# A last stage in the place of the spectral matrices: residual loaded once, columns on SBUF partitions 22 to 105, last exchange on two queues

## Chip, core and metric

The kernel runs on one core of one Trainium2 chip, as one program of some 61,000 instructions. The metric is the device time of a run in microseconds (us), the lower the better. The core has five engines that work in parallel, each from its own queue in order: PE (matrix products), DVE and ACT (element by element), POOL (the same, used here for fills and small copies) and SP (which here only issues transfers). Transfers between DRAM and SBUF, the on-chip memory of 128 partitions, are issued from SP and ACT and carried out by the core's DMA engines.

## What is computed

The input is an image of 4 x 56 x 56 positions with 128 channels. Layer 0 is group normalization, local attention over 7 x 7 windows and a residual sum. Layer 1 works on the 3136 positions of each image as a sequence t: a linear attention with a residual sum, then a sum of a spectral filter and a short autoregressive filter, again with a residual sum.

```python
x = x + conv_attention(group_norm(x))            # 7x7 windows, 4 heads
t = to_tokens(x)                                 # (4, 3136, 128)
t = t + linear_attention(layer_norm(t))
u = layer_norm(t)
# for the one scale that log_weights + gumbel select:
#   U_plus, U_minus = causal FFT convolutions of u with 16 filters phi
#   out = sum_k sigma_k^0.25 (U_plus_k Mpp_k + U_minus_k Mpm_k)
#   out = out + sum_{i<3} shifted(u, i) Mu_i
t = t + out * weight                             # cut to T // frac positions
```

The end of the kernel, which the change touches, is the last sum: the spectral part is brought back from the frequency domain to positions and added to what is there already, the residual `td`.

## The kernel before

`layers` does everything up to the spectral filter. It leaves in DRAM `td` (residual with the autoregressive part, 4 images x 3136 positions x 128 channels), `xd` (the rows of the image, transformed), the filter's values `vd` and the matrices `wd`. Its instructions are put in order by a hand-written planner; the change does not touch it.

`spectral_layer` (L1420) goes over N1 = 42 frequencies `m1`, most of them in pairs (`UNITS`), and its PE order is written out by hand (`manual_schedule`); the order on the other engines is found by the framework from what it expects to be ready, with the order of the code as priority. It keeps in a pool `sp1`, for its whole length, `mats` (16 KB a partition, L1431), `gt` (112 KB, L1441), the filter matrices of the frequencies in work, and three `us` (10.5 KB each, L1445). For each frequency it

- loads `xm` from `xd` (`load_tokens`) and makes `us` (`token_points`);
- makes the matrices of the next frequencies into `gt` (`matrices`, PE L1519, copies L1529) in turn with the products of this one (`product`, PE L1539), whose result is copied to `ys` by ACT (L1631);
- exchanges axes through DRAM (`regroup`): four stores `yd<-ys` (L1552), and after their landing four loads `yg<-yd` (L1558), all on SP's queue;
- some steps later, in `results`, transforms columns (`columns`, PE L1567), copies to `zs` with ACT and DVE (`evacuate`, L182 and L184) and stores `zd<-zs` in four transfers on SP's queue (`store_columns`, L1582).

The last frequency, 41, has nothing left to hide behind: its exchange, columns and stores are followed only by the last stage.

`onto_the_rest` (L1678) is that last stage, in a new pool `fin` and a new PSUM pool of four banks, opened when the pools of `spectral_layer` are closed. `zd` holds, for each of 56 image columns, 84 values (real and imaginary parts of 42 frequencies) x 2 x 512. The stage goes through the columns of the two halves of the image (28 each) in eleven steps of 1, 1, 2, 4, 4, 4, 4, 4, 2, 1, 1 columns. In each step and for each half `q`,

- ACT's queue loads the residual `tl<-td` (L1707), 56 rows on the partitions from 64q on, four buffers;
- SP's queue loads `z<-zd` (L1709), 84 rows on partitions 0 to 83, four pairs of buffers;
- PE multiplies with `onto` (L1717), four products a column for the two halves, over all 128 partitions; the partitions from 64 on of the z buffers are filled with zeros once before (L1695, half by DVE, half by POOL), as is `onto` (L1685);
- DVE adds the result, masked, to `tl` (L1726);
- ACT's queue stores `out_dram<-tl` (L1731).

Two lines say how a z load is laid out:

```python
z = zs[n % 4][q]
nc.sync.dma_start(z[: 2 * N1, :wc], zd[ws].rearrange("w p s b e -> p w s (b e)"))
```

Of the kernel before, what the change touches and what calls it, by code (L numbers as in the profile page):

```python
# [11 lines left out]
F32 = mybir.dt.float32  # L12
AF = mybir.ActivationFunctionType
ALU = mybir.AluOpType
AX = mybir.AxisListType

P = 128
B, H, W, C = 4, 56, 56, 128
# [39 lines left out]
NS, BR = 2, H // 2  # L58
N1, N2, NM = 42, W, W // 2
# [5 lines left out]
NSB = NS * B  # L65
# [68 lines left out]
def hybrid_kernel(  # L134
# [23 lines left out]
    nc = tc.nc  # L158
    xt = x.rearrange("b h w c -> b (h w) c")
    ot = out.rearrange("b h w c -> b (h w) c")  # L160
# [3 lines left out]
    table = {k: nc.inline_tensor(v, name=k).ap() for k, v in spectral_tables().items()}  # L164
# [1255 lines left out]
    def spectral_layer():  # L1420


        with ExitStack() as ph:
            tabs = ph.enter_context(tc.tile_pool(name="tabs", bufs=2))
            sp = ph.enter_context(tc.tile_pool(name="sp", bufs=2))
            sp1 = ph.enter_context(tc.tile_pool(name="sp1", bufs=1))
            ps_g = ph.enter_context(tc.tile_pool(name="ps_g", bufs=1, space=bass.MemoryType.PSUM))


# [118 lines left out]

            def regroup(m1, ys):

                for j in range(4):
                    nc.sync.dma_start(  # L1552
                        yd[m1, j::4].rearrange("n k e -> k n e"), ys[32 * j : 32 * (j + 1)]
                    )
                yg = sp.tile([P, NSB, C], F32, name="yg")
                for at, p, part in parts():
                    k0 = (2 * p + part) * NSB
                    nc.sync.dma_start(yg[at], yd[m1, :, k0 : k0 + NSB])  # L1558
                return yg

            def columns(m1, yg, zs, pz):
# [14 lines left out]

            def store_columns(m1, zs):
                to = zd.rearrange("(c p) r s b e -> c p r s (b e)", p=2)
                for s in range(NS):
                    for part in range(2):  # L1580
                        at = 64 * s + NM * part
                        nc.sync.dma_start(to[:, :, part * N1 + m1, s], zs[at : at + NM])  # L1582

            turn = [0]

# [22 lines left out]
            def step(s):  # L1608


                one = UNITS[s - 1] if s else []
                two = UNITS[s] if s < len(UNITS) else []
                turns = NM // 4
                free = MQ * len(one)

                order = list(range(free, NQE)) + list(range(free)) if two else []
                need = lambda t: -(-NMQ * (t + 1) // 4) if t < free else 0
                done = 0

                def make():  # L1620
                    if order and need(order[0]) <= done:
                        t = order.pop(0)
                        for n in range(len(two)):
                            matrices(s, t, n)

                def use(q, ns):

                    py = bank().rearrange("p (n c) -> p n c", c=C)
                    for i, n in enumerate(ns):
                        product(py[:, i], s - 1, us_of(one[q]), q, n)  # L1630
                    nc.scalar.copy(ys[:, ns[0] : ns[-1] + 1], py[:, : len(ns)])  # L1631

                if not one:
                    load_to(1)
                    points(0)
                    while order:
                        make()
                elif len(one) == 1 and two:
                    ys = sp.tile([P, turns, C], F32, name="ys")
                    for n in range(turns):  # L1640
                        make()
                        use(0, [n])
                        done += 1
                        if n == 3:
                            points(two[0])
                    ygs[one[0]] = regroup(one[0], ys)
                    make()
                    points(two[1])
                else:
                    waiting = list(ygs)  # L1650
                    for q in range(len(one)):
                        ys = sp.tile([P, turns, C], F32, name="ys")
                        for n in range(0, turns, 2):
                            last = n + 1 == turns
                            if last and q == 0 and two:
                                points(two[0])
                            if last and q == len(one) - 1:
                                if q:
                                    waiting.append(one[0])
                                for m1 in waiting:  # L1660
                                    results(m1)
                            use(q, [n] if last else [n, n + 1])
                            done += len(range(n, min(n + 2, turns)))
                            make()
                        ygs[one[q]] = regroup(one[q], ys)
                    if len(two) == 2:
                        points(two[1])
                assert not order

            with tc.manual_schedule(engines={mybir.EngineType.PE}):  # L1670
                for s in range(len(UNITS) + 1):
                    if s + 1 < len(UNITS):
                        tables_of(UNITS[s + 1][0])
                    step(s)
                for m1 in list(ygs):
                    results(m1)

    def onto_the_rest():  # L1678

        with ExitStack() as ph:  # L1680
            fin = ph.enter_context(tc.tile_pool(name="fin", bufs=4, reuse_waits="tile"))
            ps_o = ph.enter_context(tc.tile_pool(name="ps_o", bufs=4, space=bass.MemoryType.PSUM))

            onto = fin.tile([P, NS, 64], F32, name="onto", bufs=1)
            nc.vector.memset(onto, 0.0)  # L1685
            nc.scalar.dma_start(
                onto[: 2 * N1, :, :H], table["onto"].rearrange("p (s h) -> p s h", s=NS)
            )
            zs = [
                [fin.tile([P, 4, NS, B * C], F32, name=f"z{q}{i}", bufs=1) for q in range(2)]  # L1690
                for i in range(4)
            ]
            for i in range(4):
                for q, e in enumerate((nc.vector, nc.gpsimd)):
                    e.memset(zs[i][q][64:], 0.0)  # L1695
            rows_in = td.rearrange("b (h w) c -> h b w c", w=W)
            rows_out = ot.rearrange("b (h w) c -> h b w c", w=W)

            steps = (1, 1, 2, 4, 4, 4, 4, 4, 2, 1, 1)
            assert sum(steps) == W // 2  # L1700
            for n, wc in enumerate(steps):
                w0 = sum(steps[:n])
                tl = fin.tile([P, B, max(steps), C], F32, name="tl")
                zin = []
                for q in range(2):
                    ws = slice(q * BR + w0, q * BR + w0 + wc)
                    nc.scalar.dma_start(tl[64 * q : 64 * q + H, :, :wc], rows_in[:, :, ws])  # L1707
                    z = zs[n % 4][q]
                    nc.sync.dma_start(  # L1709
                        z[: 2 * N1, :wc], zd[ws].rearrange("w p s b e -> p w s (b e)")  # L1710
                    )
                    zin.append(z)
                for i in range(wc):
                    po = ps_o.tile([P, B, C], F32, name="po2")
                    for s in range(NS):
                        for q in range(2):
                            nc.tensor.matmul(  # L1717
                                po[64 * q : 64 * (q + 1)].rearrange("p b c -> p (b c)"),
                                onto[:, s],
                                zin[q][:, i, s],  # L1720
                                start=(s == 0),
                                stop=(s == NS - 1),
                            )
                    for q in range(2):
                        at = slice(64 * q, 64 * q + H)
                        nc.vector.scalar_tensor_tensor(  # L1726
                            tl[at, :, i], po[at], hmask[at], tl[at, :, i], ALU.mult, ALU.add
                        )
                for q in range(2):
                    ws = slice(q * BR + w0, q * BR + w0 + wc)  # L1730
                    nc.scalar.dma_start(rows_out[:, :, ws], tl[64 * q : 64 * q + H, :, :wc])  # L1731

    unfit = keep.tile([1, 1], mybir.dt.int32, name="unfit")
    layers(False, unfit)
    bad = nc.values_load(unfit)
    spectral_layer()
    onto_the_rest()
    with tc.If(bad > 0):
        layers(True, None)
        spectral_layer()  # L1740
        onto_the_rest()


# [52 lines left out]
```

## Time and profile before

| what | before |
| --- | --- |
| median of three runs | 1659.32 us (1655.94 to 1659.87) |
| the profiled execution, its own time | 1652.25 us |
| its span, first to last instruction | 1650.4 us |
| PE busy | 1452.0 us, 88% of the span |
| DVE, ACT, POOL busy | 1012.8, 753.8, 419.2 us |
| mean granted clock of PE | 0.927 |
| moved by DMA | 207.21 MB, 126 GB/s over the span |
| last product of frequency 41 (L1539) begins | 1494.86 us |
| first residual load `tl<-td` issued | 1509.41 us |
| first load `z<-zd` issued | 1516.70 us |
| PE on the last stage (L1717) | 75.1 us busy, 224 records |
| DVE's sums on the last stage (L1726) | 56 of 750 ns |

Times in the profile run from the start of the span. L1717 stands for line 1717 of the program. A group of instructions is named by engine, line and operation with out<-in by tile names. "SPq" and "ACTq" are the queues of SP and ACT, where transfers are issued; a transfer itself stands as "DMA out<-in". The chain of waits is followed back from the last instruction: at each step to what released it, or to what stood before it on its engine. A window gives, for a stretch of the span, the busy time of each engine, PE's granted clock, the mean busy share of 16 DMA engines and the bytes moved per second.

### The profile page before, as it was taken

The numbers are of one execution on the slowest core, as the hardware profiler recorded it, in microseconds if no ns is written. First come the engines' busy times: TensorE is split into PE (matmuls) and PEld (weight loads), VectorE is DVE, ScalarE is ACT, GpSimd is POOL, SyncE is SP. The second block draws the span as 40 slices with busy tenths as digits, with TensorE's granted clock in tenths as the row PEclk, the third lists the DMA queues.
The fourth block names the chain that finished last, engine by engine and source line by source line (L and its number), as shares of the span: only waits on it lengthen the run. The fifth ranks groups of instructions, "written<-read, shape, count | busy, mean of one in ns | idle before, by whom it ended". The sixth has DMA issues, their size and how long they took to land.

```text
span 1650.4 us, 61067 instructions
## 1 busy us (share of the span) xinstructions
PE 1452.0 (88%) x26361; PEld 1124.3 (68%) x26361; DVE 1012.8 (61%) x2056; ACT 753.8 (46%) x1599; POOL 419.2 (25%) x831
## 2 busy tenths in 40 slices
PE   4886888899999999884999999999999999992556
PEld 3665667766776676672888888888888888880211
DVE  4775778676876767540766666666666666642324
ACT  2342444355545544342656656565665665640000
POOL 4134326543753464340001010101010011003000
PEclk9698999899998999885999999999999999995888
DMA  6554454744434234357234345444454444435997
GB/s 174 117 103 106 87 92 107 156 119 122 120 93 126 68 113 119 86 142 189 66 99 128 104 117 136 123 116 114 122 133 111 115 123 123 113 89 142 224 262 225
DMA packets 294710, 207.21 MB, mean 126 GB/s; under 512 B 106272, under 2 KB 261376, under 8 KB 294432
## 3 DMA queue, kind: packets, MB, share of 16 engines
q1 hardware_dynamic: 281538, 189.64, 45.2%
q10 hardware_dynamic: 12894, 13.58, 3.1%
q8 instruction: 209, 3.42, 0.9%
q14 instruction: 69, 0.57, 0.1%
HBM read 115.49 MB, written 87.64 MB: 123 GB/s over the span
## 4 chain that ended last, share of the span: by engine, by line
PE 66%; DMA 13%; DVE 9%; POOL 5%; SPq 3%; issue 2%; ACT 1%; DVEq 0%; ACTq 0%; POOLq 0%
PE pg L1519 18%; PE pg L1539 17%; PE pg L1488 5%; PE results L1186 4%; PE bk L823 3%; PE scores L1156 3%; PE pg L1567 3%; PE bk L888 2%; SPq L230 2%; DVE e L1176 2%; DMA tl<-td 2%; DMA out_dram<-tl 2%; DMA z<-zd 2%; PE bk L728 2%; POOL hna L542 2%
## 5 line engine op out<-in xcount | busy, mean ns | idle before, releaser
L1529 DVE COPY gt<-pg 128x448 f32<-128x448 f32 x672 | 372.9, 617 | 225.8 <-PE pg L1519 225.7
L1529 ACT COPY gt<-pg 128x448 f32<-128x448 f32 x672 | 313.7, 555 | 100.8 <-PE pg L1519 100.5
L1519 PE MATMUL pg<-v,mats 32*128 32x224 f32 (+1 forms) x5632 | 308.4, 355 | 0.0
L1539 PE MATMUL pg<-gt,us 128*32 128x128 f32 x9408 | 297.9, 277 | 1.4 <-DVE gt L1529 1.3
L1539 PEld LDWEIGHTS pg<-gt,us 128*32 128x32 f32 x9408 | 256.4, 138 | 52.2 <-DVE gt L1529 45.4
L1519 PEld LDWEIGHTS pg<-v,mats 32*128 32x128 f32 x5632 | 250.0, 186 | 30.0 <-issue 28.2
L1500 POOL COPY us<-us 128x448 f32<-128x448 f32 x42 | 23.5, 560 | 671.8 <-DVE us L1497 611.7
L1172 ACT ACTIVATE e<-scores 126x768 f32<-126x768 f32 (+1 forms) x140 | 107.6, 768 | 113.0 <-PE scores L1156 76.1
L1176 DVE TENSOR_TENSOR e<-e,relb 126x768 f32<-126x768 f32 (+1 forms) x140 | 138.5, 990 | 23.6 <-ACT e L1172 23.2
L1200 DVE RECIPROCAL recs<-results 128x96 f32<-128x96 f32 (+1 forms) x140 | 99.5, 710 | 49.9 <-PE results L1186 48.5
L1717 PE MATMUL po<-z,onto 128*64 128x512 f32 x224 | 75.1, 720 | 59.9 <-DMA z<-zd 59.3
L1156 PEld LDWEIGHTS scores<-qT,kp 32*126 32x126 f32 (+1 forms) x2240 | 76.6, 189 | 51.3 <-ACT e L1172 24.0
L1156 PE MATMUL scores<-qT,kp 32*126 32x96 f32 (+1 forms) x2240 | 99.9, 293 | 12.4 <-ACT e L1172 12.0
L1631 ACT COPY ys<-pg 128x256 f32<-128x256 f32 (+1 forms) x171 | 58.6, 343 | 106.9 <-PE pg L1539 103.5
L1488 PE MATMUL pg<-tok,xm 56*128 56x56 f32 x1344 | 87.2, 278 | 21.7 <-DMA xm<-xd 21.7
L1488 PEld LDWEIGHTS pg<-tok,xm 56*128 56x128 f32 x1344 | 81.5, 191 | 34.9 <-issue 23.6
L1717 PEld LDWEIGHTS po<-z,onto 128*64 128x64 f32 x224 | 25.7, 162 | 110.2 <-issue 74.4
L1497 DVE COPY us<-pg 128x448 f32<-128x448 f32 x84 | 48.5, 620 | 71.7 <-PE pg L1488 71.7
L823 PE MATMUL bk<-mu,ut 128*112 128x128 f32 x672 | 87.5, 291 | 2.2 <-POOL ut L807 1.5
L1186 PE MATMUL results<-e,v_sb 126*32 126x96 f32 (+1 forms) x2240 | 77.4, 258 | 11.8 <-DVE aT L1201 11.6
L1726 DVE SCALAR_TENSOR_TENSOR tl<-po,hmask,tl 56x512 f32<-56x512 f32 x56 | 42.0, 750 | 74.1 <-PE po L1717 73.4
L823 PEld LDWEIGHTS bk<-mu,ut 128*112 128x112 f32 x672 | 82.7, 195 | 4.3 <-POOL ut L807 1.9
(175 smaller groups left out, 1942.7 us busy)
## 6 DMA issues: line engine op xcount, KB each, us to landing
xd<-xs SPq DMA_DIRECT2D x112, 168.0 KB
xm<-xd SPq DMA_DIRECT2D x168, 112.0 KB
yd<-ys SPq DMA_DIRECT2D x168, 112.0 KB
yg<-yd SPq DMA_DIRECT2D x168, 112.0 KB
zd<-zs SPq DMA_DIRECT2D x168, 112.0 KB
v_sb<-vpad SPq DMA_DIRECT2D x224, 63.0 KB
z<-zd SPq DMA_DIRECT2D x10, 1344.0 KB
acc<-in_x_dram SPq DMA_DIRECT2D x28, 224.0 KB
```

Source lines behind the costliest of these rows:

```text
L823: nc.tensor.matmul(pt[:CP, g * C : (g + 1) * C], ut[:, t0 : t0 + 2 * CP - 1 : 2], mu[:, i, :], start=(i == 0), stop=(i == NAR - 1),)
L1156: nc.tensor.matmul(sp[:, h, c * nq : (c + 1) * nq], keys_of(x0, y0 + c * KH, KH)[hs], qTs[b, ty][hs, QR * x0 : QR * x0 + nq], start=True, ...
L1172: nc.scalar.activation(e.rearrange("k (h q) -> k h q", h=NH), sp, AF.Exp)
L1176: nc.vector.tensor_tensor(e, e, relb[qc].rearrange("k h c q -> k (h c q)"), ALU.mult)
L1186: nc.tensor.matmul(po[hs, i, :nq], ones[:kn] if i else v_sb[:kn, c, hs], e[:, h, c], start=(c == 0), stop=(c == 1),)
L1200: nc.vector.reciprocal(rec, po[:, 1, :nq])
L1488: nc.tensor.matmul(pu[p][:, HALF * k : HALF * (k + 1)], xm[at, k // B, k % B, :], tok[at], start=True, stop=True,)
L1519: nc.tensor.matmul(pg[g][:, cols * i : cols * (i + 1)], mats[rows, t, ni * n + i, :], v[rows], start=True, stop=True,)
L1529: copy(rows_of(u + 1, t)[:, : MQ * nm, :, e0 : e0 + ni], pg[g][:, : cols * ni].rearrange("p (i q c) -> p q c i", i=ni, q=MQ * nm),)
L1539: nc.tensor.matmul(py[32 * j : 32 * (j + 1)], us.rearrange("p c k m -> p (c k) m")[:, NSB * FIRST[p, c] : NSB * (FIRST[p, c] + 4), 4 * n + j],
L1631: nc.scalar.copy(ys[:, ns[0] : ns[-1] + 1], py[:, : len(ns)])
L1717: nc.tensor.matmul(po[64 * q : 64 * (q + 1)].rearrange("p b c -> p (b c)"), onto[:, s], zin[q][:, i, s], start=(s == 0), stop=(s == NS - 1),)
```

## The change

The last stage becomes part of `spectral_layer`, and `onto_the_rest` goes.

- `sp1` (`mats`, `gt`, `us`) gets a stack of its own, `matrices_in`, and is closed right after the loop over the steps, before the results of the last frequencies. The pool `fin` is opened in its place, while the pools of tables, of `zs`/`yg` and the eight PSUM banks stay open.
- The residual is one tile, `rest`, of 56 KB a partition. It is loaded by fourteen transfers of four columns each, all issued on ACT's queue ahead, in the code, of the results of the last frequencies.
- `onto` and z loads lie on partitions 22 to 105 instead of 0 to 83. The z buffers are three pairs instead of four, filled with zeros whole, by POOL.
- The last stage's products take PSUM from the eight banks of `spectral_layer` (`bank()`) instead of four of their own. DVE adds into `rest`, and the stores to the output are made from it.
- For frequency 41 the exchange (`regroup`), and for 40 and 41 the stores to `zd` (`store_columns`), go half on SP's queue and half on ACT's.

The diff, cut:

```diff
-            sp1 = ph.enter_context(tc.tile_pool(name="sp1", bufs=1))
+            matrices_in = ph.enter_context(ExitStack())
+            sp1 = matrices_in.enter_context(tc.tile_pool(name="sp1", bufs=1))
...
             def regroup(m1, ys):
+                queues = (nc.sync, nc.sync if m1 < N1 - 1 else nc.scalar)
                 for j in range(4):
-                    nc.sync.dma_start(
+                    queues[j % 2].dma_start(
                         yd[m1, j::4].rearrange("n k e -> k n e"), ys[32 * j : 32 * (j + 1)]
                     )
...
-                    nc.sync.dma_start(yg[at], yd[m1, :, k0 : k0 + NSB])
+                    queues[part].dma_start(yg[at], yd[m1, :, k0 : k0 + NSB])
...
+                queues = (nc.sync, nc.sync if m1 < N1 - 2 else nc.scalar)
...
-                        nc.sync.dma_start(to[:, :, part * N1 + m1, s], zs[at : at + NM])
+                        queues[part].dma_start(to[:, :, part * N1 + m1, s], zs[at : at + NM])
...
+            matrices_in.close()
+            fin = ph.enter_context(tc.tile_pool(name="fin", bufs=1, reuse_waits="tile"))
...
+            rest = fin.tile([P, B, BR, C], F32, name="rest")
+            half = [slice(64 * q, 64 * q + H) for q in range(2)]
+            for w0 in range(0, BR, 4):
+                for q in range(2):
+                    nc.scalar.dma_start(
+                        rest[half[q], :, w0 : w0 + 4], rows_in[:, :, q * BR + w0 : q * BR + w0 + 4]
+                    )
+            among = slice(P // 2 - N1, P // 2 + N1)
+            onto = fin.tile([P, NS, 64], F32, name="onto")
+            nc.gpsimd.memset(onto, 0.0)
+            nc.scalar.dma_start(
+                onto[among, :, :H], table["onto"].rearrange("p (s h) -> p s h", s=NS)
+            )
+            DEEP = 3
+            zin = [
+                [fin.tile([P, 4, NS, B * C], F32, name=f"z{q}{i}") for q in range(2)] for i in range(DEEP)
+            ]
+            for zs in zin:
+                for z in zs:
+                    nc.gpsimd.memset(z, 0.0)
+            with tc.manual_schedule(engines={mybir.EngineType.PE}):
                 for m1 in list(ygs):
                     results(m1)
...
             for n, wc in enumerate(steps):
...
                     nc.sync.dma_start(
-                        z[: 2 * N1, :wc], zd[ws].rearrange("w p s b e -> p w s (b e)")
+                        zin[n % DEEP][q][among, :wc],
+                        zd[q * BR + w0 : q * BR + w0 + wc].rearrange("w p s b e -> p w s (b e)"),
                     )
...
-                    po = ps_o.tile([P, B, C], F32, name="po2")
+                    po = bank()
...
-                            tl[at, :, i], po[at], hmask[at], tl[at, :, i], ALU.mult, ALU.add
+                            rest[half[q], :, w0 + i],
+                            po[half[q]].rearrange("p (b c) -> p b c", b=B),
+                            hmask[half[q]],
+                            rest[half[q], :, w0 + i],
+                            ALU.mult,
+                            ALU.add,
...
-                    nc.scalar.dma_start(rows_out[:, :, ws], tl[64 * q : 64 * q + H, :, :wc])
+                    nc.scalar.dma_start(
+                        rows_out[:, :, q * BR + w0 : q * BR + w0 + wc], rest[half[q], :, w0 : w0 + wc]
+                    )
```

More of the change, by code (lines that the diff above doesn't have):

```diff
@@ L1674, in spectral_layer @@
                     step(s)
+            matrices_in.close()
+            fin = ph.enter_context(tc.tile_pool(name="fin", bufs=1, reuse_waits="tile"))
+            rows_in = td.rearrange("b (h w) c -> h b w c", w=W)
+            rows_out = ot.rearrange("b (h w) c -> h b w c", w=W)
+            rest = fin.tile([P, B, BR, C], F32, name="rest")
[5 more added lines that the diff above has]
+                    )
@@ L1675, in spectral_layer @@
+            with tc.manual_schedule(engines={mybir.EngineType.PE}):
                 for m1 in list(ygs):
                     results(m1)
[L1678 to L1697, printed above, removed]
@@ L1699, in onto_the_rest @@
             steps = (1, 1, 2, 4, 4, 4, 4, 4, 2, 1, 1)
-            assert sum(steps) == W // 2
+            assert sum(steps) == BR
             for n, wc in enumerate(steps):
                 w0 = sum(steps[:n])
-                tl = fin.tile([P, B, max(steps), C], F32, name="tl")
-                zin = []
                 for q in range(2):
-                    ws = slice(q * BR + w0, q * BR + w0 + wc)
-                    nc.scalar.dma_start(tl[64 * q : 64 * q + H, :, :wc], rows_in[:, :, ws])
-                    z = zs[n % 4][q]
@@ L1709, in onto_the_rest @@
                     nc.sync.dma_start(
-                        z[: 2 * N1, :wc], zd[ws].rearrange("w p s b e -> p w s (b e)")
+                        zin[n % DEEP][q][among, :wc],
+                        zd[q * BR + w0 : q * BR + w0 + wc].rearrange("w p s b e -> p w s (b e)"),
                     )
-                    zin.append(z)
                 for i in range(wc):
-                    po = ps_o.tile([P, B, C], F32, name="po2")
+                    po = bank()
                     for s in range(NS):
@@ L1717, in onto_the_rest @@
                             nc.tensor.matmul(
-                                po[64 * q : 64 * (q + 1)].rearrange("p b c -> p (b c)"),
+                                po[64 * q : 64 * (q + 1)],
                                 onto[:, s],
-                                zin[q][:, i, s],
+                                zin[n % DEEP][q][:, i, s],
                                 start=(s == 0),
@@ L1724, in onto_the_rest @@
                     for q in range(2):
-                        at = slice(64 * q, 64 * q + H)
                         nc.vector.scalar_tensor_tensor(
-                            tl[at, :, i], po[at], hmask[at], tl[at, :, i], ALU.mult, ALU.add
+                            rest[half[q], :, w0 + i],
[4 more added lines that the diff above has]
+                            ALU.add,
                         )
                 for q in range(2):
-                    ws = slice(q * BR + w0, q * BR + w0 + wc)
-                    nc.scalar.dma_start(rows_out[:, :, ws], tl[64 * q : 64 * q + H, :, :wc])
+                    nc.scalar.dma_start(
+                        rows_out[:, :, q * BR + w0 : q * BR + w0 + wc], rest[half[q], :, w0 : w0 + wc]
+                    )
     unfit = keep.tile([1, 1], mybir.dt.int32, name="unfit")
@@ L1736, in hybrid_kernel @@
     spectral_layer()
-    onto_the_rest()
     with tc.If(bad > 0):
@@ L1740, in hybrid_kernel @@
         spectral_layer()
-        onto_the_rest()
 def kernel(**inputs):
```

## The prediction

> **What bounds the kernel now.** I read the page first (where in the span the DMA engines are full), then the chain of waits from 1494 us on, then the waits of SP's queue and a table of windows over the last stage. The two slice rows of the page (40 slices of 41 us) show the last stage, slices 38 to 40, as the one stretch where the DMA engines are full; there PE is not (its last four digits are 2, 5, 5, 6).
>
> ```profile
> span 1650.4 us, 61067 instructions
> DMA  6554454744434234357234345444454444435997
> GB/s 174 117 103 106 87 92 107 156 119 122 120 93 126 68 113 119 86 142 189 66 99 128 104 117 136 123 116 114 122 133 111 115 123 123 113 89 142 224 262 225
> ```
>
> The chain of waits (start, length, what) shows how that stage begins: column 41's exchange through DRAM, link by link, most of it on SP's queue, with the DMA engines mostly idle.
>
> ```profile
> 1495.83 0.83 SPq L1582
> ...
> 1499.28 0.48 SPq L1552
> ...
> 1500.80 2.07 DMA yd<-ys
> ...
> 1503.39 2.60 DMA yg<-yd
> ...
> 1506.13 3.16 PE pg L1567 x8
> ...
> 1510.15 0.84 SPq L1582
> ...
> 1512.71 3.70 DMA zd<-zs
> ```
>
> The windows (start:end, length, busy per engine, granted clock, DMA share, GB/s) show what the transfers reach. From 1497 to 1510, during that exchange, it is 106. From 1517 on they are full, but at very different speeds: loads alone (1527:1537) 211; residual loads alone (1556:1558, no z load is in flight then) 158; loads and stores together (1580:1600, 1610:1616) about 300.
>
> ```profile
> 1497.00:1510.00 13.00, 3.11 (x8) 0.61 (x8) 0.63 (x1) 0.72 (x2) 0.53 (x1) 0.62 0.41 106
> 1527.00:1537.00 10.00, 5.59 (x16) 1.96 (x16) 5.71 (x5) 0.00 (x0) 0.00 (x0) 0.81 0.91 211
> 1556.00:1558.00 2.00, 2.00 (x12) 0.95 (x10) 1.50 (x2) 0.00 (x0) 0.00 (x0) 1.00 0.91 158
> 1558.00:1560.00 2.00, 2.00 (x12) 0.72 (x8) 1.68 (x3) 0.00 (x0) 0.00 (x0) 1.00 0.93 223
> 1580.00:1600.00 20.00, 15.97 (x51) 5.11 (x50) 11.23 (x15) 0.00 (x0) 0.00 (x0) 1.00 0.90 300
> 1610.00:1616.00 6.00, 6.00 (x20) 2.11 (x19) 3.86 (x6) 0.00 (x0) 0.00 (x0) 0.77 0.90 304
> ```
>
> SP's own waits (who waits for whom: total us, times, longest) show that z loads are held back by transfers they have no data from. In the trace eight DMA semaphores are taken in turn, and an issue waits until the former user of its semaphore has landed.
>
> ```profile
> SPq L1709 <- DMA tl<-td: 42.8, 5, 16.0
> SPq L1709 <- DMA out_dram<-tl: 33.6, 6, 9.7
> SPq L1709 <- DMA z<-zd: 29.3, 6, 8.9
> ```
>
> So the last stage is bound by bytes towards SBUF. The page's DMA issues give them: z<-zd 10x1344 + 8x336 + 4x672 KB = 19.27 MB; tl<-td and out_dram<-tl each 10x448 + 8x112 + 4x224 KB = 6.42 MB. Loads are 25.69 MB. From the first tl issue at 1509.41 to the landing of the last z load at 1641.9 that is 132.5 us, 194 GB/s on average; from there to the span's end 8.5 us pass.
>
> [...] two queues together, share 0.90 to 0.93, no more than one alone. [...]
>
> **The change, part by part.** The sum is made against the profiled execution: span 1650.4 of 1652.25 us, so 1.85 lie around it; the median of the three runs, 1659.32, is 7.07 above it. I carry a difference in span over to the median unchanged.
>
> Nothing before 1495 changes: columns up to 39 keep SP alone.
>
> *Two queues for columns 40 and 41.* Of four issues each, two go to ACT. From the chain: L1582 at 1495.83, two issues less of 0.80, 1.7 us; L1552, two of 0.46, 1.0 us; L1558, two of 0.38, at most 0.8; L1582 at 1510.15, 1.7 us. At best 5.1 us. But ACT's part only counts if nothing stands ahead of it, and the residual load does (next).
>
> *Residual: 14 loads of 448 KB on ACT instead of 22.* They need the place of the matrices; its last reader is the product L1539, done at 1496.8 (timeline: 1494.86 + 1.94). ACT gets to them after its ys copy (1497.14), its two zd stores (2 x 0.8) and yd stores (2 x 0.46), at once or after waiting for yd: 1498 to 1502, I take 1500; before it was 1509.41. Fourteen issues at the 0.43 us median of L1707 are 6 us of ACT's queue, and with eight semaphores they stretch over the transfer. What is queued behind on ACT: the zs copy of column 41, half of its yg loads perhaps, and half of its zd stores; for these SP's z loads wait. In the order of readiness the residual goes first, as tl(0) went ahead of the onto load that precedes it in the code. Rate: between the 158 and 223 of the windows 1556:1558 and 1558:1560 (estimate 190), so 6.42 MB take 34 us (29 to 41), to 1534.
>
> *Then column 41's rest and the z loads.* If yg came through early, only the zd stores stand behind the residual: 0.8 + the landing, about 2.5 us. If the yg loads stand behind it too, the chain's columns, copy, two issues, landing remain: 3.2 + 0.7 + 1.7 + 3.7 + gaps 0.4 = 9.7 us. I take 4: z starts at 1538 instead of 1516.7, but with no residual left to load.
>
> *z loads on the middle partitions.* In 1580:1600 four stores of 448 KB pass (two issued at 1563.8, two at 1585.1), 1.84 MB or 92 GB/s, which leaves 208 of 300 for loads; alone they made 211. So 200 to 223, value 207: 19.27 MB take 93 us (86 to 96). I price the move of the partitions itself at nothing: packets of one z load lengthen alike over all rows in the trace's packet records (about 250 ns per 4 KB, where an undisturbed one takes 159)[...]. Its bound on the good side is the 300 GB/s seen for everything: 25.69 MB of z and stores in 86 us, 7 less than 93. A loss is excluded: the same bytes, rows and engines[...].
>
> *Stores* stay behind the z loads of later steps: 92 GB/s beside 208 needs 6.42 MB in 70 us of those 93. If that cover were gone they would cost up to 21 us (6.42 MB at 300).
>
> *Edits at nothing.* Memsets: six whole tiles on POOL at 3.51 us (same free size as L1695's) end at 1497 + 21 = 1518, under the residual load; if z could start at 1512, the third buffer's load would wait up to 6 us. DVE loses 4 x 3.47 us, of which PE waited 1.2. Three z buffers instead of four: PE needs 75.1/28 = 2.7 us a column, 10.7 a step, less than the 13.3 us of a step's z (2.75 MB at 207). PSUM from eight banks instead of four: DVE's 1.5 us a column is the shorter. After the change a step has four transfers instead of six on the eight semaphores, so two steps are in flight: this is why I take 207 and not 194.
>
> *Tail.* As before, 8.5 us from the last z landing.
>
> Sum: 1500 + 34 + 4 + 93 + 8.5 = 1639.5, against 1650.4: 10.9 us less. On the median: **1648**.
>
> **The rivals.**
> *A (forecast, 0.50):* as summed; with the ends, 1498 + 29 + 2.5 + 86 + 8.5 = 1624 to 1502 + 41 + 8 + 96 + 8.5 = 1655.5, so 1633 to 1664 on the median.
> *B, the middle partitions lift the z rate (0.24):* z and stores run together at 300: 1538 + 86 + 8.5 = 1632.5, so 1641. For: one half alone at 158, and 300 was reached. Against: the even lengthening of packets.
> *C, slower (0.17): the last exchange is stuck behind the residual.* yg and zd of column 41 wait on ACT until the residual has landed at the one-half rate of 158: 1502 + 40.6 + 9.7 + 96 + 8.5 = 1656.8, so 1666. It decides from a z start of about 1549 on (1641.9 - 93). For: ACT's order; against: yd and yg come first in the code.
> *D, the place comes free no earlier (0.09):* the new pool waits for the phase's last reader at 1509.3, as tl did: 1509.4 + 34 + 93 + 8.5 = 1645, so 1654.
>
> **How the numbers follow.** 0.3%, about what a measurement of this kernel can tell from no change, is 5 us. A is faster by more in 0.36, within in 0.10, slower in 0.04; B 0.23, 0.01, 0; C 0, 0.05, 0.12; D 0.05, 0.04, 0. Together 0.64, 0.20, 0.16. The range 1633 to 1665 takes in A's bounds and the nearer part of B, C and D and leaves out about 2 in 10.
>
> **What would show it.** Right: the first residual issue on ACT at 1498 to 1502 and its last landing near 1534; the first z issue near 1538; loads at about 207 GB/s afterwards; no wait of SP for residual transfers once z runs. Wrong: z windows at 280 or more with loads alone (B); z issued after 1549 (C); a first residual issue after 1509 (D); DVE's sums waiting for stores of an earlier step, since all now lie in one tile: each of five large steps would then pay a store's 16 us, and everything above falls.

## The result, and the profile after

| | before | changed |
| --- | --- | --- |
| median | 1652.97 us (1647.12 to 1659.87, 8 runs) | 1641.26 us (1637.71 to 1650.87, 8 runs) |
| ratio | 1 | 0.9935 [0.9906, 0.9964] |
| profiled execution, its own time (span) | 1652.25 us (1650.4) | 1650.87 us (1649.1) |
| last product begins | 1494.86 us | 1496.44 us |
| first residual load issued | 1509.41 us | 1500.01 us |
| first z load issued | 1516.70 us | 1539.20 us |
| last z load landed | 1641.9 us | 1638.5 us |

The change makes the kernel 0.65% faster, 10.7 us by the ratio. The profiled execution of the changed kernel is the slowest of its eight, 9.6 us above their median, so its span is no measure of the change; a second profile, of an execution nearer to the median, stands with the experiments.

The two slice rows of the page, after. Slice 37, which holds the last exchange, now moves 170 GB/s instead of 142, with the engines at 7 tenths instead of 5: the residual load fills the exchange. Slice 38, where z and residual loads ran before, now holds the end of the residual load, the start of z and a gap between them, and moves 215 instead of 224; the last two move 263 and 214 instead of 262 and 225.

```profile
span 1649.1 us, 61031 instructions
DMA  6454454644434244348244345444444444437897
GB/s 173 106 110 107 90 94 108 144 116 129 118 90 131 69 113 115 96 127 202 62 105 125 108 110 133 128 122 106 121 126 127 106 125 116 122 85 170 215 263 214
```

The timeline from the last product on (start, length, engine, line, what, and in brackets the idle time before it and what ended that).

```profile
1500.01 0.56 ACTq L1689 DMA_DIRECT2D rest<-td  x1
...
1507.05 14.56 ACTq L1689 DMA_DIRECT2D rest<-td  x12
1509.76 2.85 PE L1570 MATMUL pg<-yg,back 56*64 56x512 f32 x8 [11.38 <-DMA yg<-yd]
1512.75 0.69 DVE L184 COPY zs<-pg 128x512 f32<-128x512 f32 x1 [15.41 <-DMA rest<-td]
...
1524.20 0.59 ACT L182 COPY zs<-pg 128x512 f32<-128x512 f32 x1 [23.94 <-DMA rest<-td]
1525.55 5.16 ACTq L1586 DMA_DIRECT2D zd<-zs  x2
1527.74 5.15 SPq L1586 DMA_DIRECT2D zd<-zs  x2
1539.20 1.92 SPq L1716 DMA_DIRECT2D z<-zd  x4
```

Column 41's columns are done at 1512.6 and DVE copies its half of zs at once. ACT copies the other half at 1524.20, 11.5 us later: ACT's queue is in order, and ahead of the copy stand the fourteen residual issues and that of onto, most of which wait for DMA semaphores (the last five are issued 2.1 to 2.2 us apart, the third and fourth 0.5). Then the four zd stores are issued 2.2 us apart on two queues, each waiting for a semaphore that a residual load holds. So z starts at 1539.20. The chain says the same, and SP's waits show no wait of a z load for a residual load (the 24.2 us are zd stores):

```profile
1512.34 17.53 DMA rest<-td
1529.89 9.02 DMA zd<-zs
1541.60 13.79 DMA z<-zd
```

```profile
SPq L1716 <- DMA z<-zd: 54.9, 9, 8.0
SPq L1716 <- DMA out_dram<-rest: 29.6, 4, 13.6
SPq L1586 <- DMA rest<-td: 24.2, 2, 20.7
```

Windows 5 to 25 us after z's start (almost only z loads) and over the mixed loads and stores:

```profile
1544.20:1564.20 20.00, 12.27 (x34) 3.67 (x33) 6.00 (x8) 0.00 (x0) 0.00 (x0) 0.93 0.91 224
1580.00:1600.00 20.00, 14.96 (x42) 4.47 (x41) 6.00 (x8) 0.00 (x0) 0.00 (x0) 0.93 0.90 260
```

At this point my theory (T) was: the gain is the residual moved into the idle exchange, the rows give nothing, since 224 lies near the 211 of before, and the second queue neither helps nor hurts. The second and the third fell.

### The profile page after: what moved, and what is told of

Read it like the earlier page. It is cut to its first block, busy times and chain, and to the rows that moved or that the text cites. A ratio compares the mean times of both kernels' runs of the same rounds, so it can differ in the third digit from the quotient of the medians.

```text
span 1649.1 us, 61031 instructions
## 1 busy us (share of the span) xinstructions
PE 1453.4 (88%) x26361; PEld 1124.3 (68%) x26361; DVE 998.4 (61%) x2051; ACT 754.2 (46%) x1599; POOL 427.4 (26%) x834
## 4 chain that ended last, share of the span: by engine, by line
PE 66%; DMA 13%; DVE 7%; POOL 5%; SPq 4%; issue 2%; ACT 1%; ACTq 1%; DVEq 0%; POOLq 0%
PE pg L1521 18%; PE pg L1541 17%; PE pg L1490 5%; DMA z<-zd 4%; PE bk L823 4%; SPq L230 4%; PE results L1186 4%; PE scores L1156 3%; PE pg L1570 3%; PE bk L888 2%; PE bk L496 2%; DVE e L1176 2%; PE bk L728 1%; POOL hna L542 1%; DMA m_raw<-in_M_minus_dram 1%
## 5 line engine op out<-in xcount | busy, mean ns | idle before, releaser
L1724 PE MATMUL pg<-z,onto 128*64 128x512 f32 x224 | 76.6, 672 | 52.0 <-DMA z<-zd 51.9
L1490 PEld LDWEIGHTS pg<-tok,xm 56*128 56x128 f32 x1344 | 81.5, 191 | 35.3 <-issue 23.9
L1724 PEld LDWEIGHTS pg<-z,onto 128*64 128x64 f32 x224 | 24.8, 152 | 104.6 <-issue 87.0
L1732 DVE SCALAR_TENSOR_TENSOR rest<-pg,hmask,rest 56x512 f32<-56x512 f32 x56 | 42.0, 750 | 87.4 <-PE pg L1724 86.7
```

The lines of the kernel that those rows point to most:

```text
L1490: nc.tensor.matmul(pu[p][:, HALF * k : HALF * (k + 1)], xm[at, k // B, k % B, :], tok[at], start=True, stop=True,)
L1724: nc.tensor.matmul(po[64 * q : 64 * (q + 1)], onto[:, s], zin[n % DEEP][q][:, i, s], start=(s == 0), stop=(s == NS - 1),)
```

## The experiments

All twelve in one table. Ratios are to the kernel before, with 95% intervals; "us" is the ratio less 1, times 1652.65 us (the median of the kernel before over the 75 runs of the first set, a0 to e3). "By the ratios" below means a difference of this column; several kernels were run on different chips, each beside the kernel before. The last four columns come from each one's profile: from the start of the last product to the first z issue, from there to the landing of the last z load, from there to the end, and the rate 5 to 25 us after z's start. Where a residual load is also in flight then, the rate is in brackets.

| kernel | median us | ratio | us | to z | z | tail | GB/s |
| --- | --- | --- | --- | --- | --- | --- | --- |
| before | 1652.97 | 1 | 0 | 21.8 | 125.2 | 8.5 | (226) |
| b0, before again | 1651.05 | one run | | 21.5 | 127.7 | 8.1 | (209) |
| changed | 1641.26 | 0.9935 [0.9906, 0.9964] | -10.7 | 42.8 | 99.3 | 10.6 | 224 |
| a0, changed again | 1641.94 | 0.9934 [0.9913, 0.9955] | -10.9 | 44.3 | 97.7 | 8.9 | 247 |
| e1, rows from 0 | 1648.67 | 0.9978 [0.9958, 0.9999] | -3.6 | 42.7 | 101.3 | 8.4 | 220 |
| e2, SP's queue only | 1637.15 | 0.9902 [0.9881, 0.9923] | -16.2 | 39.8 | 95.1 | 8.6 | 252 |
| e3, 41 off ACT | 1648.48 | 0.9988 [0.9968, 1.0008] | -2.0 | 28.0 | 115.5 | 9.2 | (226) |
| e4, before with middle rows | 1646.98 | 0.9959 [0.9942, 0.9977] | -6.8 | 21.9 | 123.4 | 8.8 | (221) |
| e5, exchange off ACT | 1635.28 | 0.9912 [0.9880, 0.9944] | -14.5 | 39.3 | 94.2 | 9.0 | 243 |
| e6, e5 with rows from 0 | 1642.67 | 0.9943 [0.9922, 0.9964] | -9.4 | 40.4 | 100.5 | 8.2 | 221 |
| e7, residual with z | 1642.99 | 0.9958 [0.9940, 0.9977] | -6.9 | 26.1 | 109.9 | 10.8 | (246) |
| e8, residual in two parts | 1635.92 | 0.9880 [0.9828, 0.9932] | -19.8 | 35.7 | 98.8 | 10.1 | (245) |
| e9, small steps | 1632.70 | 0.9849 [0.9797, 0.9901] | -25.0 | 39.3 | 89.3 | 10.8 | 252 |
| e10, place alone | 1644.35 | 0.9956 [0.9938, 0.9973] | -7.3 | 40.7 | 100.8 | 8.3 | 221 |

**The changed kernel again (a0).**

> The changed kernel once more, beside the next three, for a profile nearer to its median (its first profile was the slowest of its eight runs). All theories: 1641 us, within 4; first z load near 1539, first residual load near 1500; loads alone about 210 GB/s.

The time is as in the first set, and z starts 44.3 us after the last product instead of 42.8. The profile (its lines are numbered one less) is of an execution at 1643.74 us, and its z loads run at 247 GB/s, not at the 224 of the first profile, nor near the 210 that was expected:

```profile
1540.40:1560.40 20.00, 14.62 (x38) 4.30 (x35) 6.00 (x8) 0.00 (x0) 0.00 (x0) 0.88 0.91 247
```

So the first profile had caught an execution with slow loads. Why the same program loads at 224 in one execution and at 247 in another is not settled.

**Rows from 0 (e1).**

```diff
-            among = slice(P // 2 - N1, P // 2 + N1)
+            among = slice(0, 2 * N1)
```

> The changed kernel with onto and the z loads back on partitions 0 to 83. Theory T (the gain is the residual's earlier load and fewer transfers on eight semaphores; the partitions give nothing): 1641 us, within 3 of the changed kernel on the same chip, and loads of z alone at 205 to 215 GB/s as in the kernel before. Rival M [...]: 1650 or more, and z loads alone below 200 GB/s.

6.7 us slower than the changed kernel by the medians, 7.3 by the ratios; the intervals don't meet. T fell on this point; of rival M, by which the rows bring the gain, the 1650 and the rate below 200 were too much the other way. One window of e1:

```profile
1543.70:1563.70 20.00, 13.65 (x35) 4.00 (x35) 6.00 (x8) 0.00 (x0) 0.00 (x0) 0.84 0.91 220
```

The share of busy DMA engines is 0.91 in both, so with the middle rows each transfer takes less time: 247 against 220 GB/s. In the packet records a 4 KB packet of these z loads takes 234 ns on average in a0 and 263 ns in e1.

**One part alone: middle rows in the kernel before (e4), and e5 with rows from 0 (e6).** The rows alone are changed, in two other kernels; in e4 the z buffers are also filled with zeros whole.

> The kernel before with one part of the change alone: onto and the z loads on partitions 22 to 105 (z buffers filled with zeros whole). Theory T (the partitions give nothing): within 2 us of the kernel before. Rival M (the partitions give 5 to 7 us, as the 6.7 us between the changed kernel and its version with rows from 0 would have it): 5 to 7 us faster.

> The version with the exchange off ACT, with rows 0 to 83 in place of 22 to 105. Theory T: within 2 us of it. Rival M: 5 to 7 us slower than it.

The sizes are those of rival M both times: 6.8 us in the kernel before, 5.1 (by the medians 7.4) in the version with the exchange off ACT. The second alone would not be enough, as the intervals of e5 and e6 overlap. The windows of e5 and e6 at the same distance from z's start:

```profile
1531.00:1551.00 20.00, 15.35 (x39) 4.79 (x38) 6.00 (x8) 0.00 (x0) 0.00 (x0) 0.86 0.91 243
```

```profile
1535.50:1555.50 20.00, 14.18 (x37) 4.42 (x36) 6.00 (x8) 0.00 (x0) 0.00 (x0) 0.84 0.91 221
```

Low rows give 220, 221 and 221 GB/s (e1, e6, e10), middle rows 243 to 252 (a0, e2, e5, e9), with the one exception above. From 221 to 247 is 12%. 19.27 MB take 87 us at 221 and 78 at 247; part of that time stores are mixed in, and 5 to 9 us are what four pairs of kernels show (e1 and a0, e4 and the kernel before, e6 and e5, e10 and e2). What it is about rows 22 to 105 that makes the loads faster is not shown: no third place, such as rows 44 to 127, was tried.

**SP's queue only (e2).**

```diff
-                queues = (nc.sync, nc.sync if m1 < N1 - 1 else nc.scalar)
+                queues = (nc.sync, nc.sync)
...
-                queues = (nc.sync, nc.sync if m1 < N1 - 2 else nc.scalar)
+                queues = (nc.sync, nc.sync)
```

> The changed kernel with all of the exchange of columns 40 and 41 back on SP's queue. Theory T: within 3 us of the changed kernel; ACT's zs copy of column 41 still stands behind fourteen residual issues that wait for semaphores, so z still starts near 1537 (1532 to 1540). Rival Q (the second queue gives the gain): 5 us or more slower than the changed kernel, z start 1543 or later.

5.3 us faster than a0 by the ratios, 4.8 by the medians of 22 runs each: the second queue costs. (The two intervals overlap slightly; from the 22 runs of each, taken on the same chip, the means differ by 4.9 us, with a 95% interval of 1.7 to 7.7.) Rival Q has the sign wrong. T has z's start about right, but not that the time stays, nor the reason: the copy of column 41 no longer waits behind the residual. The timeline of e2:

```profile
1489.32 25.08 ACTq L1689 DMA_DIRECT2D rest<-td  x14
...
1491.65 5.80 SPq L1555 DMA_DIRECT2D yd<-ys  x4
...
1512.72 3.39 PE L1570 MATMUL pg<-yg,back 56*64 56x512 f32 x8 [23.56 <-DMA yg<-yd]
...
1516.15 0.59 ACT L182 COPY zs<-pg 128x512 f32<-128x512 f32 x1 [26.64 <-PE pg L1570]
...
1517.02 3.66 SPq L1586 DMA_DIRECT2D zd<-zs  x4
1527.01 2.53 SPq L1716 DMA_DIRECT2D z<-zd  x6
```

The last product begins at 1487.23. In the changed kernel the second queue does shorten the first half of the exchange: the columns begin 13.3 us after the last product, here 25.5, because SP's yd issues wait for semaphores (one of them of a residual load; four issues take 5.8 us) and then share the engines with seven residual loads instead of two (from the end of the yd issues to the first yg issue pass 7.0 us instead of 4.7). But here ACT is through with its fourteen issues (at 1514.4) when the columns are done, the copy waits for PE alone, and the four stores go out at once. z starts 39.8 us after the last product, against 42.8 and 44.3.

In both kernels z starts at about the time when the last residual load lands (1526.6 here, 1537.9 in the changed kernel), and up to there both move the same 8.3 MB, at 209 GB/s here and at 194 in the changed kernel. There the residual comes out more slowly: its first load is issued 3.6 us after the last product instead of 2.1, as ACT has two zd stores of column 40 to issue first, and its third 7.0 us after its first instead of 1.0, as ACT's yd stores and its yg loads, which wait for yd to land, stand between. The rest of the 5.3 us lies in z, 95.1 against 97.7 and 99.3; what it is due to was not tried.

**Column 41 off ACT (e3), and the whole exchange off ACT (e5).** In e3 both zs copies of column 41 go to DVE and its zd stores to SP; e5 is e2 with these copies and with the load of onto on SP, ahead of the residual in the code.

```diff
-                    evacuate(zs[:, p], pz[p])
+                    if m1 == N1 - 1:
+                        nc.vector.tensor_copy(zs[:, p], pz[p])
+                    else:
+                        evacuate(zs[:, p], pz[p])
```

> The changed kernel with column 41's zs copies both on DVE and its four zd stores on SP, so that nothing of column 41 stands behind the residual on ACT after its yg loads. Theory T: zs copies near 1514, zd stores then wait only for semaphores held by residual loads, z starts at 1522 to 1530 instead of 1539; the bytes are the same and the DMA engines were full until 1534, so only the gap of 1534 to 1542 is won: 1636 us, 2 to 8 less than the changed kernel. Rival S (the end follows z's start one for one): 10 to 16 us less, 1625 to 1631. Rival N (zd is held by semaphores anyway): z start still after 1535, time the same.

z starts 28.0 us after the last product, 15 earlier than in the changed kernel, and yet the time is 6.5 us longer by the medians. T has z's start, but none of T, S and N the time. The timeline of e3 shows part of what took it back:

```profile
1507.31 1.29 DVE L1579 COPY zs<-pg 128x512 f32<-128x512 f32 x2 [16.78 <-PE pg L1570]
...
1517.61 32.20 SPq L1719 DMA_DIRECT2D z<-zd  x8
1530.74 0.86 ACTq L1700 DMA_DIRECT2D onto<-onto  x1
1545.34 5.25 PE L1727 MATMUL pg<-z,onto 128*64 128x512 f32 x12 [38.12 <-DMA onto<-onto]
```

PE waited for onto, a load of 84 x 448 bytes: it stood on ACT behind all fourteen residual issues, and the residual now ran beside z. From issue to PE's start pass 14.6 us. Meanwhile all z buffers were full, and from 1545 to 1549 no byte moved. The larger part is something else: seven of the fourteen residual loads, all of which the changed kernel has behind it when z starts, landed only after z's start here. They are 2.9 MB, some 14 us at the 209 GB/s of that stretch (1517.6 to 1544.9). So z takes 115.5 us instead of 97.7 to 99.3, and most of the early start was bytes put off.

> The changed kernel with nothing of the exchange on ACT: its four groups of transfers on SP only, column 41's zs copies both on DVE, and the small load of onto on SP ahead of yg instead of behind fourteen residual loads. Theory T (bytes over the rate once the DMA engines are kept busy): the 5 us hole that the late onto load tore into the version with 41 off ACT is gone, z starts 26 to 30 us after the last product, the stage from the last product to the end takes 138 to 143 us against 143.5 with SP alone and 151 to 153 in the changed kernel; 1630 to 1636 us. Rival N (z's start is worth nothing): as with SP alone, 1637.

1635.3 us is in T's range, and the stage takes 142.5 us, but not in T's way: z starts 39.3 us after the last product, not 26 to 30, as the exchange on SP alone crawls beside the residual, as in e2 (the columns begin 23.9 us after the last product, in e2 25.5). Against e2 the intervals overlap, so rival N is not excluded. The two queues of e3 together with an early onto were not tried.

**The residual with z (e7).** e5, with the residual loads moved in the code behind the results of column 41, and this ahead of them:

```diff
+            nc.vector.tensor_copy(rest[:, 0, ::4, 0], zs[:, 0, : BR // 4])
```

> The version with the exchange off ACT, but no residual load begins before column 41's zs copy is done (one small DVE copy into the residual's tile from zs, overwritten by the loads, makes them wait). Theory T (what the early residual gains is the bytes that the exchange leaves unmoved): residual begins some 22 us after the last product instead of 3, about 15 us in which 150 GB/s more could pass are lost, 2.2 MB or 9 us at 245 GB/s: 7 to 11 us slower than the version with the exchange off ACT. Rival E (the early residual only crowds the exchange): the exchange gets 3 to 5 us shorter without it and the time changes by less than 4 us.

7.6 us slower than e5 by the ratios, as T has it, though the intervals just overlap (in the profiles the stage from the last product to the end is 4.3 us longer). The exchange does get shorter (z starts at 26.1 instead of 39.3), but the bytes are only put off: z takes 109.9 instead of 94.2 us. So the early residual is worth some 4 to 8 us, although it delays z by 13.

**The residual in two parts (e8).** e5 with six loads ahead and eight held as in e7.

> The version with the exchange off ACT, with six residual loads (2.7 MB) ahead of column 41's exchange and the other eight held until its zs copy is done. Theory T (the gap of the exchange is filled, and its stores find free semaphores): z starts 24 to 30 us after the last product instead of 39, and the residual's second part shares the engines with z, so stores begin earlier and more of the loads pass beside stores; 137 to 141 us from the last product to the end, 1629 to 1634 us. Rival B (only bytes over the rate of loads count): no gain, 1635 to 1638 us.

No difference from e5 can be told (1635.92 against 1635.28; by the ratios 5.3 us, with intervals that overlap widely). z starts at 35.7, as the six loads hold up yd on SP and then leave the engines idle (a share of 0.11 from 1517 to 1522). T's way failed (z's start, and 144.6 us from the last product to the end). The median lies in rival B's range, the ratio (-19.8 us) in T's, so the time decides nothing.

**Small steps (e9).**

```diff
-            steps = (1, 1, 2, 4, 4, 4, 4, 4, 2, 1, 1)
+            steps = (1, 1) + 12 * (2,) + (1, 1)
...
-            DEEP = 3
+            DEEP = 6
```

(on e5, with z tiles of two columns)

> The version with the exchange off ACT, with fourteen steps of 1, 1, 2 (twelve times), 1, 1 columns and six pairs of z buffers of half the size (the same place). Theory T: the hole near the end (9 of 16 engines busy for 5 us, z's issue waits for PE's last use of a buffer of four columns) is gone, 3 to 5 us; 1630 to 1633 us. Rival S (eight semaphores: eight transfers of half the size keep only half the bytes in flight, and each issue waits for a landing): 3 us or more slower, 1638 to 1645 us.

The kernel has sixteen steps (the expectation miscounts them as fourteen). 1632.7 us, 0.9849 [0.9797, 0.9901], faster than the kernel before and the changed kernel; against e5 the intervals overlap, so what small steps bring by themselves is not settled. Rival S's 3 us slower is not seen. The hole of e5 was there (a share of 0.59 from 1611 to 1616), but T had its cause only in part: by the trace the z load due then waited 1.9 us for PE's buffer and the next one 8 us, until 1614.8, for the semaphore of an output store. With small steps the mixed phase runs at 308 GB/s instead of 290. Windows of e5, then of e9:

```profile
1561.00:1601.00 40.00, 31.41 (x99) 10.26 (x98) 17.41 (x24) 0.00 (x0) 0.00 (x0) 0.96 0.90 290
...
1611.00:1616.00 5.00, 5.00 (x25) 1.95 (x24) 4.37 (x6) 0.00 (x0) 0.00 (x0) 1.00 0.59 216
```

```profile
1573.00:1613.00 40.00, 33.88 (x112) 10.62 (x111) 21.00 (x28) 0.00 (x0) 0.00 (x0) 1.00 0.91 308
```

**The place alone (e10)**, e2 with rows from 0, closes a ladder of one edit a rung, and **the kernel before again (b0)** gives a second profile.

> The changed kernel with rows 0 to 83 and SP's queue only: of the change, the place of the matrices and the residual loaded at once are left (with the smaller edits: three pairs of z buffers, eight PSUM banks). With it each step from the kernel before to the changed kernel is one edit: place, then rows (the version with SP's queue only), then the second queue. Theory T' (the three add up: place -8 to -9, rows -6 to -7, second queue +4 to +5): 1643 to 1645 us. Rival I (they don't add up: with low rows the place brings little, as 4 us between the kernel before and the changed kernel with rows from 0 would have it): 1647 to 1650 us.

> The kernel before once more, for a second profile of its last stage. The medians lie 11 us apart, but the stage from the last product to the end was 155.5 us in its first profile and 150.9 and 152.7 in two of the changed kernel. Theory V (the stage varies by some us between executions, and the first profile caught a short one): 157 to 162 us here. Rival F (part of the 11 us is won before the last product): 154 to 157 again.

1644.35 us is in the range of T', though the interval of the place (4.5 to 10.2 us less) does not quite exclude I. By the ratios the rungs are: place -7.3 us (with the smaller edits), rows -8.9, second queue +5.3. That they sum to the -10.9 of a0 is so by construction. The test is in the other kernels: rows alone (e4, -6.8) and place alone (-7.3) make -14.1, and e2, which has both, -16.2; place and second queue make -2.0, and e1 has -3.6. So the three add up within the noise. In b0 the stage from the last product to the end took 157.2 us, at the lower edge of what V expects: before 155.5 and 157.2, changed 152.7 and 150.9. The profiles thus show some 5 of the 11 us. The order of the instructions ahead of column 40's stores is the same on every engine in all these kernels, and the last product begins anywhere from 1486.6 to 1498.7 us; two profiles each can't settle the other 6, and sizes here rest on the medians. Nothing speaks for rival F: on average the last product begins at 1492.3 us in the three profiles of the kernel before and e4, and at 1492.7 in the eleven others.

## Why the prediction was right, and where it was not

The predicted change, -10.9 us, is what was measured (-10.7 by the ratio, -11.7 by the medians); the predicted time, 1648, lies 7 us too high because the three runs shown (1659.32) were above the kernel's usual time (1652.97 over eight runs, 1652.65 over 75). That the sum came out right is luck: it took all of the 10.9 us from the new place and nothing from the rows and the second queue, where the runs show -7.3, -8.9 and +5.3.

- *Residual from 1500, z from 1538:* 1500.01 and 1539.20, right as times, but by two errors that cancel. The load took 37.9 us (39.6 in a0) instead of 34, and the remaining exchange 1.3 instead of 4, since the zd stores land with the last residual loads rather than after them. The 158 GB/s taken for residual loads alone (window 1556:1558) did not come back: from 1510 to 1530, when nothing else moved, the residual ran at 204 to 207. (The window 1558:1560 with 223, the other end of that estimate, held 47 GB/s of output stores.)
- *"I price the move of the partitions itself at nothing":* this step failed. It is worth 5 to 9 us in four pairs of runs. That packets lengthen alike over all rows was taken as evidence against; the records name no row of a packet, and the rate nevertheless rises by 12% (221 to 247 GB/s) on rows 22 to 105. Rival B had the direction, with a size (300 GB/s for everything) that no run reached over the whole stage.
- *Two queues, "at best 5.1 us" saved:* the sum took nothing from it, and it costs 5.3. The text named the condition, that nothing stands ahead on ACT, but did not price its failure, nor that ACT's part of the exchange in turn holds up the residual. Rival C named half of the mechanism, with z at 1549 or later: column 41's copy and zd stores did wait behind the residual, its yg loads did not, and z started at 1539.
- *z in 93 us at 207 GB/s beside 92 of stores:* mis-sized. With the rows of before (e10) z takes 100.8 us. I had taken 300 GB/s for loads and stores together from the window 1580:1600; over the whole mixed phase it is 257 in the kernel before and 258 in e10:

```profile
1561.00:1632.00 71.00, 43.66 (x130) 13.39 (x127) 24.34 (x33) 0.00 (x0) 0.00 (x0) 0.88 0.90 257
```

```profile
1563.00:1625.00 62.00, 48.87 (x142) 15.33 (x140) 25.88 (x35) 0.00 (x0) 0.00 (x0) 0.89 0.90 258
```

  So the place alone brings 7.3 us, not 10.9.
- *Memsets and the single residual tile at nothing:* right. POOL's six memsets end at 1519.4, under the residual load; DVE's 56 sums take 750 ns each as before and wait for PE, not for stores. Three pairs of z buffers instead of four were not tried alone.

## What to carry to other kernels

When a stage is bound by transfers, measure its rate over the whole stage in question and not in its best window, and look at which partitions a load fills: moving 84 rows from partitions 0 to 83 to partitions 22 to 105 was worth about as much (5 to 9 us) as moving 6.4 MB into an idle stretch (7 us). Ahead of bulk loads on an in-order queue, list what is issued behind them there, the small load (PE had it 14.6 us after its issue in e3) and the copy that someone waits for (11.5 us late in the changed kernel) above all, and what stands among them and waits itself, and count the DMA semaphores that the bulk load holds (SP's zd stores waited 24.2 us for them). A second queue that shares these with a bulk load can cost more than it saves (5.3 us here).

## What the runs showed of the hardware

- With the same share of busy DMA engines (0.90 to 0.91) loads ran at 220 to 221 GB/s on rows 0 to 83 and at 243 to 252 on rows 22 to 105 (224 in one execution), loads and stores together at up to 308 (e9).
- A load of 84 x 448 bytes behind fourteen residual loads of one queue took 14.6 us until PE could use it (e3).
- The changed kernel loaded z at 224 GB/s in one execution and at 247 in another; what makes the difference is open.
